# A four-layer graph network on one core: the scheduler learns of a shared port, the score weights read their vectors from PSUM, and bias times degree moves

## The chip, the cores and the metric

The kernel runs on one core of one Trainium2 chip. The metric is the time of one execution on the device in microseconds (us), from the start of the program to its end; the median of several executions counts. The engines of the core are TensorE (PE in the profile, with its weight loads as PEld), VectorE (DVE), ScalarE (ACT) and GpSimd (POOL). All DMAs of this kernel are issued by SyncE (SP). Each engine takes its instructions strictly in the order in which the program lists them.

## The reference

The input x holds 128 graphs of 64 nodes with 512 features, so 8192 rows. All graphs share one 64 x 64 adjacency. Four layers follow one another, and each adds its result to x and normalizes:

```
x = layernorm(x + L0(x)); x = layernorm(x + L1(x)); x = layernorm(x + L2(x)); x = layernorm(x + L3(x))

L0:  mi = x @ Wi.T;  mj = x @ Wj.T
     out = deg * (mi + b) + adj @ mj                       # deg = row sums of adj

L1:  four heads, each:  Wh = x @ W_heads[h]
     e[n, m] = leaky(Wh[n] . a1 + Wh[m] . a2), masked by adj; attn = softmax(e); h = elu(attn @ Wh)
     the four h are concatenated to 2048 features; one more such attention with W_out, a_out; elu
     ffn = relu(out @ w1 + b1) @ w2 + b2;  layernorm(ffn + out) * gamma + beta

L2, L3:  Wh = x @ W;  e = leaky(Wh @ a_src [n] + Wh @ a_dst [m]), masked; out = softmax(e) @ Wh
```

The scores never need Wh: Wh . a equals x . (W a). The kernel works out the vectors W a once, and calls them score weights.

## The kernel before

**Tiles and pairs.** 128 rows (two graphs) are one tile, and two tiles are a pair p. There are 32 pairs (NP), and each goes through all layers. Pairs are staggered, so that PE finds work of several pairs at any time. Matrix products of pair 4 and later are done as seven half-size products (`seven`, `strassen`), with the sums that this needs made by GpSimd and VectorE, and with weight parts streamed from DRAM into rings of buffers. The first four pairs (AHEAD) do layer 0 with plain matmuls instead, named `l` in the profile, since the streamed parts (`raw_w`, `raw_wo`, `raw_W`, made by `stage_stream`) are not ready yet.

**How the order is made.** No instruction is issued while the stages run. Each stage is a Python generator. `start(at, order, stage)` puts it on a heap, keyed by a nominal time in which one pair takes TURN = 107, and what it yields is added to its time. Every call such as `nc.vector.tensor_tensor` is only recorded by `Plan.note` (line 174) as a `Step`: its engine, its rank (place of recording), the steps it must follow, and the tiles it opens. Then `Plan.order` (line 207) runs a list scheduler over all steps. It keeps one clock for each engine, takes a duration for each step from `cost` (line 319), gives an engine the ready step with the lowest rank, and lets a step that opens a tile wait until a buffer of its tag is free. `play` (line 301) issues all steps in that order. So every instruction has the same line in the profile, L306, and a changed duration in `cost` can move any instruction of any engine, all on their in-order queues. The line that the reduces get, and the one of GpSimd:

```
    if name == "tensor_tensor_reduce":
        return 0.78, 0.0
    if engine == "gpsimd":
        return 0.25 + 0.0026 * size, 0.0
```

**PSUM.** One pool with one tag "b" and eight buffers, one bank each, serves all PSUM tiles.

**The start.** The adjacency is loaded, then the first x tile, the first quarter of W0T (two DMAs), the second x tile, the bias row spread over the partitions (`degb`), and the other quarters of W0T. VectorE works out `deg`, multiplies `degb` by it, makes masks, and builds `aggr`, the block matrix through which PE forms x times adjacency transposed (`axp`), in which an identity scaled by deg is folded. ScalarE copies `axp` to `ax`, GpSimd adds `degb` to x, PE does the `l` matmuls with `ax` and `w0`, VectorE adds them to x (`x<-l`), and `normalize` follows: `bn_stats` and `bn_aggr` on VectorE (`st`, `mv`), two small GpSimd steps (`rs`), one VectorE step (`sh`), one ScalarE step on x.

**Score weights of the heads.** `score_weights` (line 474) goes over the four heads h, the two score vectors s and the four row chunks c. Each step is a `tensor_tensor_reduce` on VectorE: a 128 x 512 chunk of the head's weights (`wh`) times the vector, spread over the partitions (`rows_a`), summed into one column of `wa_h`; its full product goes to `j_h`, which nobody reads. In the profile this operation is called CUSTOM_DVE_ANT_0, and DVE_READ_ACCUMULATOR2_ANT fetches its sum. After each head `head_sums` makes the four sums of `wh` on GpSimd, in place. `wa_h` is then used twice: by PE for the scores of the first two pairs (`fp`, from a transposed x, `x1Tp` and `x1T`), and by `score_rows`, which turns it over and stores it as rows in DRAM for the later pairs. The scores of layers 2 and 3 get theirs in the same way from `stage_score_rows`, as `j<-w,rows_a`, one "head" each.

**After the scores.** `attention_heads` forms the attention: `dg` on VectorE, `bc` on PE, a row of VectorE steps and one exponential on ScalarE, `pt` on PE, `aT` on ScalarE. PE multiplies x by it (`yp`), forms the head products (`stx_h`, `sty_h`) into `hT`, and later the product with W_out (`stx_o`, `sty_o`, parts `ws_wo` loaded from DRAM). The remaining stages follow in the same manner; the last pair uses `stage_last` and `stage_tile` with plain matmuls (`hidp`, `gp`, `yp`).

Of the kernel before, what the change touches and what calls it, by code (L numbers as in the profile page):

```python
# [12 lines left out]
FP = mybir.dt.float32  # L13
# [3 lines left out]
ALU = mybir.AluOpType  # L17
AX = mybir.AxisListType
PSUM = bass.MemoryType.PSUM

P = 128
# [120 lines left out]
class Step:  # L142
    def __init__(self, engine, rank):
        self.engine, self.rank = engine, rank
        self.calls, self.after, self.behind = [], set(), set()
        self.opens, self.uses = [], set()
        self.takes, self.lands = 0.0, 0.0


class Plan:  # L150
# [23 lines left out]
    def note(self, engine, name, args, kw):  # L174
        if self.joined:
            s = self.joined[0]
            assert s.engine == engine
        else:
            s = Step(engine, len(self.steps) - self.early)
            self.steps.append(s)  # L180
            if self.joined is not None:
                self.joined.append(s)
        out = [kw[k] for k in ("out", "accum_out") if k in kw] + (
            [] if "out" in kw or not args else [args[0]]
        )
        views = [(v, True) for v in out if isinstance(v, View)] + [
            (v, False)
            for v in [*args, *kw.values()]
            if isinstance(v, View) and not any(v is o for o in out)
        ]  # L190
        for v, writes in views:
            t = v.tile
            writes = writes or t.pool.space is PSUM
            if not t.seen:
                s.opens.append(t)
            else:
                s.behind.add(t.seen[0][0])
            s.uses.add(t)
            s.after.update(o for o, r, w in t.seen if (w or writes) and v.meets(r))
            t.seen.append((s, v.region, writes))  # L200
        s.after.discard(s)
        s.behind -= {s} | s.after
        s.calls.append((name, args, kw))
        takes, s.lands = cost(engine, name, args, kw, out)
        s.takes += takes

    def order(self):

        engines = ("tensor", "vector", "scalar", "gpsimd", "sync")
        free = dict.fromkeys(engines, 0.0)  # L210
        coming = {e: [] for e in engines}
        there = {e: [] for e in engines}
        wire, out = 0.0, []
        then = {s: [] for s in self.steps}
        for i, s in enumerate(self.steps):
            s.no, s.ready, s.waits = i, 0.0, len(s.after) + len(s.behind)
            for o in s.after:
                then[o].append((s, True))
            for o in s.behind:
                then[o].append((s, False))  # L220
            for t in s.uses:
                t.left += 1
            s.given = set()
            for k in set(t.slots for t in s.opens):
                k.openers.append(s)
        for k in set(t.slots for s in self.steps for t in s.opens):
            k.openers.sort(key=lambda s: -s.no)

        def late(s, e):
            return 0.0 if s.engine == e else WAIT + SLACK.get(s.engine, 0.3)  # L230

        def come(s):
            heapq.heappush(coming[s.engine], (s.ready, s.rank, s.no, s))

        def take(slots):

            while slots.queue:
                s = slots.queue[0][1]
                while slots in slots.openers[-1].given:
                    slots.openers.pop()  # L240
                if s.no > slots.openers[-1].no + NEAR:
                    return
                n = sum(t.slots is slots for t in s.opens)
                if len(slots.free) < n:
                    return
                heapq.heappop(slots.queue)
                s.given.add(slots)
                for _ in range(n):
                    end, _, last = heapq.heappop(slots.free)
                    s.ready = max(s.ready, end + late(s, None))  # L250
                    if last:
                        s.after.update(o for o, _, _ in last.seen)
                s.waits -= 1
                if not s.waits:
                    come(s)

        def want(s):

            kinds = {id(t.slots): t.slots for t in s.opens}.values()
            s.waits = len(kinds)  # L260
            if not kinds:
                come(s)
            for k in kinds:
                heapq.heappush(k.queue, (s.no, s))
            for k in kinds:
                take(k)

        for s in self.steps:
            if not s.waits:
                want(s)  # L270
        while len(out) < len(self.steps):
            at, e = min(
                (free[e] if there[e] else max(free[e], coming[e][0][0]), e)
                for e in engines
                if there[e] or coming[e]
            )
            while coming[e] and coming[e][0][0] <= at:
                s = heapq.heappop(coming[e])[3]
                heapq.heappush(there[e], (s.rank, s.no, s))
            s = heapq.heappop(there[e])[2]  # L280
            s.start, s.end = at, at + s.takes
            free[e] = s.end
            if s.lands:
                wire = max(wire, at) + s.lands
                s.end = wire + 2.0
            out.append(s)
            for o, whole in then[s]:
                t = s.end + late(o, None if s.lands else e) if whole else at
                o.ready = max(o.ready, t)
                o.waits -= 1  # L290
                if not o.waits:
                    want(o)
            for t in s.uses:
                t.left -= 1
                t.end = max(t.end, s.end)
                if not t.left:
                    heapq.heappush(t.slots.free, (t.end, t.no, t))
                    take(t.slots)
        return out
# [16 lines left out]
        return lambda *args, **kw: self.plan.note(self.name, call, args, kw)  # L316


def cost(engine, name, args, kw, out):

    size = max(math.prod(v.shape[1:]) for v in out) if out and isinstance(out[0], View) else 512
    if engine == "tensor":
        if name == "transpose":
            return size * 0.00085, 0.0

        beside = P * P // math.prod(kw["lhsT"].shape)
        return (
            size * 0.00169 if beside == 1 else 0.208 / beside + 0.0003 * size
        ), 0.0
    if engine == "sync":  # L330
        return 0.06, 0.0015 * size
    if name == "tensor_tensor_reduce":
        return 0.78, 0.0
    if engine == "gpsimd":
        return 0.25 + 0.0026 * size, 0.0
    return 0.17 + (0.0011 if engine == "vector" else 0.00085) * size, 0.0


# [1 line left out]
def gnn_stack_kernel(  # L340
# [24 lines left out]
    nc = Plan(tc)  # L365
    NT, D = x.shape
# [15 lines left out]
    psum = nc.pool(ctx, name="ps", bufs=8, space=PSUM)  # L382
# [32 lines left out]
    for k in range(KC):  # L415
        for s in range(2):
            nc.sync.dma_start(out=w0[s][:, k, :], in_=W0T[ts(s * KC + k, P), :])
        if k == 0:
            nc.sync.dma_start(out=xs[0][:, 1, :], in_=x[P : 2 * P, :])
            degb = row(b0, "degb")  # L420
# [17 lines left out]
    nc.vector.tensor_copy(adj_f, adj_i)  # L438
    deg = cp.tile([P, 1], FP, tag="deg", name="deg")
    nc.vector.tensor_reduce(deg, adj_f, AX.X, ALU.add)  # L440
    nc.vector.tensor_scalar(degb, degb, deg, None, ALU.mult)
    mask1 = cp.tile([P, N], I32, tag="mask1", name="mask1")
    nc.vector.tensor_scalar(mask1, adj_f, 0.0, None, ALU.is_le)
    mask2 = cp.tile([P, N], I32, tag="mask2", name="mask2")
# [17 lines left out]

    nc.vector.tensor_tensor(aggr[:, 1, 0, :], aggr[:, 0, 0, :], aggr[:, 0, 1, :], ALU.add)
    nc.vector.tensor_copy(aggr[:, 1, 1, :], aggr[:, 0, 1, :])


    aTg = [cp.tile([P, T, P], FP, tag=f"aTg{i}", name=f"aTg{i}") for i in range(2)]
# [6 lines left out]
    def score_weights(Ws, avecs, name, then=lambda h: None):  # L474

        n = len(Ws)
        wa = cp.tile([P, 2 * n, KC], FP, tag=f"wa_{name}", name=f"wa_{name}")
        for h in range(n):
            for s in range(2):
                for c in range(KC):  # L480
                    junk = unit.tile([P, D], BF, tag="junk", name=f"j_{name}_{s}_{h}_{c}")
                    nc.vector.tensor_tensor_reduce(
                        junk, Ws[h](c), avecs[h][:, s, :], 1.0, 0.0, ALU.mult, ALU.add,
                        accum_out=wa[:, s * n + h, c : c + 1],
                    )
            then(h)
            yield 5.0
        was[name] = wa
# [19 lines left out]
    for h in range(H):  # L508
        w = wp.tile([P, KC // 2, 7, D // 2], FP, tag=f"wh{h}", name=f"wh{h}")
        for s in range(2):  # L510
            nc.sync.dma_start(
                out=w[:, :, 2 * s : 2 * s + 2, :].rearrange("p c h o -> p c (h o)"),
# [734 lines left out]
    for p in range(NP):  # L1247
        if p < AHEAD:
            start(TURN * (0.2 * p - 1.2), 10 * p + 4, stage_first(p))
        else:  # L1250
# [4 lines left out]
        at, pace, rest = {NP - 2: (2.0, 0.8, 0.0), NP - 1: (1.3, 0.6, 0.0)}.get(  # L1255
            p, (1.42, 1.0, 5.0)
        )
# [76 lines left out]
```

## Time and profile before

| | us |
|---|---|
| median of 3 executions | 3350.42 (3348.55 to 3352.29) |
| the profiled execution, its own time | 3351.91 |
| its span | 3350.1 |
| PE busy | 3284.4 (98%) |
| DVE busy | 2432.1 (73%) |
| POOL busy | 1714.0 (51%) |
| ACT busy | 1356.2 (40%) |

The profiled execution took 1.8 us more than its span, and 1.5 us more than the median. The mean granted clock of PE was 0.992 of full speed. Busy time is summed for each engine over the whole span; idle time of an engine matters only where the end of the program waits for it. A group "out<-in x32 | 32.9, 1028" has 32 instructions that were busy for 32.9 us together, 1028 ns each in the mean; after the next bar stands the idle time just before them and what ended it.

### The profile page before, as it was taken

The page shows a single profiled execution, that of the slowest core. Times are in us where ns is not written, and L with a number is a line of the kernel's source. Part 1 is how long each engine was busy: PE and PEld are TensorE (multiplying, and loading weights), DVE is VectorE, ACT ScalarE, POOL GpSimd, SP SyncE. Part 2 cuts the span into 40 slices and gives each one's busy share as a digit, 9 for nine tenths or more (in the row PEclk, how much of TensorE's full clock was granted, in tenths as well). Part 3 has the DMA queues.
Part 4 walks back from the last instruction along what each step waited for, and adds up shares of the span by engine and source line. Part 5 has one row for each costly group of instructions (what it writes and reads, how often), then busy time and mean ns, then how long its engine had stood idle before and what let it go on. Part 6 is the DMA issues. An engine that isn't in the chain of part 4 may idle for free.

```text
span 3350.1 us, 59710 instructions
## 1 busy us (share of the span) xinstructions
PE 3284.4 (98%) x21298; PEld 2891.1 (86%) x21298; DVE 2432.1 (73%) x5698; ACT 1356.2 (40%) x3184; POOL 1714.0 (51%) x1860
## 2 busy tenths in 40 slices
PE   8899999999999999999999999999999999999997
PEld 4788988888988888989889889889888889889884
DVE  6757777777777777777776777777777777777756
ACT  1343444434443443443443443444444344434332
POOL 6754455554455554555544555544555544555432
PEclk9999999999999999999999999999999999999998
DMA  8766666666666676666676666666666666666751
GB/s 282 269 217 204 203 216 223 217 224 211 210 213 220 213 227 215 202 219 219 213 232 205 206 222 217 219 218 211 213 217 217 222 212 209 215 220 209 241 190 60
DMA packets 301063, 718.08 MB, mean 214 GB/s; under 512 B 32560, under 2 KB 41824, under 8 KB 300768
## 3 DMA queue, kind: packets, MB, share of 16 engines
q1 hardware_dynamic: 300768, 714.27, 66.2%
q8 instruction: 171, 2.80, 0.3%
q14 instruction: 124, 1.02, 0.1%
HBM read 680.82 MB, written 33.32 MB: 213 GB/s over the span
## 4 chain that ended last, share of the span: by engine, by line
PE 92%; DMA 3%; DVE 3%; issue 1%; SPq 1%; POOL 1%; ACT 0%; POOLq 0%; DVEq 0%
PE stx_h L306 13%; PE stx_o L306 13%; PE stx L306 12%; PE sty_h L306 10%; PE sty_o L306 10%; PE sty L306 9%; PE hidp L306 6%; PE yp L306 4%; PE gp L306 3%; PE stx_y L306 3%; PE sty_y L306 2%; PE axp L306 2%; PE bc L306 1%; PE op L306 1%; PE oTp L306 1%
## 5 line engine op out<-in xcount | busy, mean ns | idle before, releaser
L306 DVE CUSTOM_DVE_ANT_0 j<-x,rows 128x512 bf16<-128x512 f32 x736 | 610.2, 829 | 73.3 <-ACT x L306 36.4
L306 PE MATMUL stx_h<-ys,wh 128*128 128x128 f32 x3072 | 405.6, 276 | 2.1 <-DVE hT L306 1.6
L306 PEld LDWEIGHTS stx_h<-ys,wh 128*128 128x128 f32 x3072 | 386.7, 192 | 22.6 <-issue 9.0
L306 ACT COPY hT<-stx_h 128x256 f32<-128x256 f32 x384 | 143.0, 372 | 498.4 <-PE stx_h L306 491.4
L306 POOL TENSOR_SCALAR rs<-mv 128x1 f32<-128x1 f32 x256 | 85.5, 334 | 394.5 <-DVE mv L306 376.0
L306 ACT ACTIVATE x<-x,sh,rs 128x512 f32<-128x512 f32 x256 | 207.7, 814 | 179.0 <-DVE sh L306 177.4
L306 PE MATMUL sty_h<-ys,wh 128*128 128x128 f32 x2048 | 274.5, 277 | 0.0
L306 DVE TENSOR_TENSOR x<-stx,x 128x256 f32<-128x256 f32 x360 | 150.1, 418 | 155.6 <-PE stx L306 154.4
L306 PEld LDWEIGHTS sty_h<-ys,wh 128*128 128x128 f32 x2048 | 251.6, 192 | 12.3 <-issue 5.7
L306 PE MATMUL sty_o<-ws_wo,hT 128*128 128x256 f32 x1024 | 245.9, 383 | 6.6 <-DMA ws_wo<-d_wo 6.6
L306 PE MATMUL stx_o<-ws_wo_T,s_o 128*128 128x256 f32 x1024 | 244.5, 382 | 0.2 <-DVE who L306 0.2
L306 POOL TENSOR_TENSOR ys<-ys,t 128x256 f32<-128x256 f32 x128 | 113.0, 885 | 256.5 <-PE sty_h L306 256.3
L306 PE MATMUL hidp<-oT,w 128*128 128x256 f32 (+1 forms) x1056 | 231.8, 373 | 0.0
L306 DVE TENSOR_TENSOR hT<-sty_h,hT 128x256 f32<-128x256 f32 x256 | 107.8, 421 | 168.0 <-PE sty_h L306 141.3
L306 PEld LDWEIGHTS sty_o<-ws_wo,hT 128*128 128x128 f32 x1024 | 189.2, 191 | 32.3 <-issue 3.9
L306 PEld LDWEIGHTS hidp<-oT,w 128*128 128x128 f32 x1056 | 192.8, 190 | 23.7
L306 PEld LDWEIGHTS stx_o<-ws_wo_T,s_o 128*128 128x128 f32 x1024 | 185.7, 190 | 26.1 <-DVE who L306 2.6
L306 ACT ACTIVATE elu<-hT 128x512 f32<-128x512 f32 x256 | 153.3, 601 | 104.2 <-DVE hT L306 92.8
L306 DVE SCALAR_TENSOR_TENSOR hT<-elu,hT 128x512 f32<-128x512 f32 x256 | 173.0, 682 | 28.2 <-ACT elu L306 25.1
L306 DVE BATCH_NORM_STATS2 st<-x 128x6 f32<-128x512 f32 x256 | 176.3, 689 | 5.4
L306 POOL TENSOR_TENSOR rs<-rs,mhalf 128x1 f32<-128x1 f32 x256 | 154.2, 602 | 21.3
L306 ACT COPY ys<-yp 128x512 f32<-128x512 f32 x256 | 131.2, 606 | 82.8 <-PE yp L306 73.9
(199 smaller groups left out, 7706.6 us busy)
## 6 DMA issues: line engine op xcount, KB each, us to landing
ws_wo_T<-d_wo_T SPq DMA_DIRECT2D x256, 512.0 KB, 3.9
ws_wo<-d_wo SPq DMA_DIRECT2D x192, 512.0 KB, 3.6
ws_W_T<-d_W_T SPq DMA_DIRECT2D x248, 256.0 KB, 3.7
rows<-d_h SPq DMA_DIRECT2D x240, 256.0 KB, 4.3
ws_w_T<-d_w_T SPq DMA_DIRECT2D x112, 512.0 KB, 4.2
ws_W<-d_W SPq DMA_DIRECT2D x186, 256.0 KB, 3.6
ws_w<-d_w SPq DMA_DIRECT2D x84, 512.0 KB, 4.3
rows<-d SPq DMA_DIRECT2D x128, 256.0 KB, 4.6
```

The costliest lines, as they stand in the source:

```text
L306: getattr(getattr(self.tc.nc, s.engine), name)(*map(real, args), **{k: real(v) for k, v in kw.items()})
```

## The change

Four things are changed.

1. The scheduler gets a port. A VectorE step that reads more than one operand from SBUF is marked, and so is a GpSimd step that does so and writes more than two elements in each partition. In `order`, a marked step starts no earlier than the port is free, and holds the port for its duration. Only the order is made with this: no instruction waits for anything on account of it.
2. Durations in `cost`: 0.7 for a reduce, and 0.2 + 0.0021 x size for GpSimd. `size_of` is the old expression under a name.
3. The multiplication of `degb` by `deg` is recorded after `aggr` is built.
4. In `score_weights` two PSUM tiles are opened for all heads, one for each s. Before the four reduces of a head and an s, ScalarE copies the vector into its tile, and the reduces read it there. These are 8 copies for the heads and 2 each for layers 2 and 3.

```diff
@@ class Step @@
-        self.calls, self.after, self.behind = [], set(), set()
+        self.calls, self.after, self.behind, self.port = [], set(), set(), False
@@ Plan.note @@
         takes, s.lands = cost(engine, name, args, kw, out)
+        if engine in ("vector", "gpsimd"):
+
+            both = [v for v, writes in views if not writes and v.tile.pool.space is not PSUM]
+            s.port = len(both) > 1 and (engine == "vector" or size_of(out) > 2)
         s.takes += takes
@@ Plan.order @@
-        wire, out = 0.0, []
+        wire, port, out = 0.0, 0.0, []
...
             s = heapq.heappop(there[e])[2]
+            if s.port and port > at:
+                at = port
+            if s.port:
+                port = at + s.takes
             s.start, s.end = at, at + s.takes
@@ cost @@
+def size_of(out):
+    return max(math.prod(v.shape[1:]) for v in out) if out and isinstance(out[0], View) else 512
...
     if name == "tensor_tensor_reduce":
-        return 0.78, 0.0
+        return 0.7, 0.0
     if engine == "gpsimd":
-        return 0.25 + 0.0026 * size, 0.0
+        return 0.2 + 0.0021 * size, 0.0
@@ gnn_stack_kernel @@
     nc.vector.tensor_reduce(deg, adj_f, AX.X, ALU.add)
-    nc.vector.tensor_scalar(degb, degb, deg, None, ALU.mult)
...
     nc.vector.tensor_copy(aggr[:, 1, 1, :], aggr[:, 0, 1, :])
+    nc.vector.tensor_scalar(degb, degb, deg, None, ALU.mult)
@@ score_weights @@
+        inps = [psum.tile([P, D], FP, tag="b", name=f"a_{name}_{s}") for s in range(2)]
         for h in range(n):
             for s in range(2):
+                a = inps[s]
+                nc.scalar.copy(a, avecs[h][:, s, :])
                 for c in range(KC):
                     junk = unit.tile([P, D], BF, tag="junk", name=f"j_{name}_{s}_{h}_{c}")
                     nc.vector.tensor_tensor_reduce(
-                        junk, Ws[h](c), avecs[h][:, s, :], 1.0, 0.0, ALU.mult, ALU.add,
+                        junk, Ws[h](c), a, 1.0, 0.0, ALU.mult, ALU.add,
                         accum_out=wa[:, s * n + h, c : c + 1],
                     )
```

All instructions of the changed kernel are issued at its line 314.

## The prediction

> **What bounds the kernel now.** I read the page's busy shares and chain first:
>
> ```profile
> span 3350.1 us, 59710 instructions
> ...
> PE 3284.4 (98%) x21298; PEld 2891.1 (86%) x21298; DVE 2432.1 (73%) x5698; ACT 1356.2 (40%) x3184; POOL 1714.0 (51%) x1860
> ...
> PE 92%; DMA 3%; DVE 3%; issue 1%; SPq 1%; POOL 1%; ACT 0%; POOLq 0%; DVEq 0%
> ```
>
> PE is idle for 65.7 us in all. The table of busy time by stretch says where:
>
> ```profile
> core 0: us, PE busy (x) PEld busy (x) DVE busy (x) ACT busy (x) POOL busy (x), PEclk, DMA share, GB/s
> 0.00:50.00 50.00, 38.89 (x185) 21.50 (x185) 28.58 (x68) 9.66 (x16) 26.40 (x33) 1.00 0.96 330
> 50.00:100.00 50.00, 40.62 (x127) 21.77 (x128) 34.97 (x56) 9.06 (x19) 39.33 (x32) 0.85 0.59 208
> 100.00:150.00 50.00, 41.01 (x375) 38.33 (x374) 39.38 (x66) 23.38 (x51) 40.76 (x25) 0.94 0.83 285
> ...
> 400.00:3200.00 2800.00, 2798.02 (x18465) 2499.89 (x18465) 2074.74 (x4902) 1166.91 (x2739) 1434.79 (x1576) 1.00 0.68 216
> ...
> 3300.00:3350.00 50.00, 33.87 (x122) 22.36 (x121) 24.12 (x75) 13.08 (x32) 9.94 (x21) 0.78 0.11 39
> ```
>
> From 400 to 3200 PE idles 2.0 us, at full clock. Nothing that VectorE gains there can shorten the span. The first 150 us hold 11.1 + 9.4 + 9.0 = 29.5 us of idle, and lose more by a clock of 0.85 and 0.94. The last 150 hold about 29. So this change can act on the head, hardly on the tail. What PE waits for in the head (the waits of PE, 0 to 150: total, times, longest):
>
> ```profile
> PE bc L306 <- DVE dg L306: 5.3, 1, 5.3
> ...
> PE sty_o L306 <- DMA ws_wo<-d_wo: 3.7, 1, 3.7
> PE fp L306 <- DVE wa_h L306: 3.7, 4, 2.4
> ```
>
> wa_h is what the score weights write. VectorE's timeline shows the two other facts that matter (start, length, what, and the idle time before it):
>
> ```profile
> 10.30 0.49 DVE L306 TENSOR_SCALAR degb<-degb,deg 128x512 f32<-128x512 f32 x1 [4.46 <-DMA degb<-in_b_dram]
> 10.70 0.25 DVE L306 TENSOR_SCALAR aggr<-ident,deg 128x64 f32<-128x64 f32 x1
> ...
> 34.95 0.69 DVE L306 CUSTOM_DVE_ANT_0 j_h<-wh,rows_a 128x512 bf16<-128x512 f32 x1
> ...
> 42.14 0.68 DVE L306 TENSOR_TENSOR x<-l,x 128x512 f32<-128x512 f32 x1
> ...
> 55.18 1.63 DVE L306 CUSTOM_DVE_ANT_0 j_h<-wh,rows_a 128x512 bf16<-128x512 f32 x1
> ```
>
> First, VectorE sits 4.46 us in front of degb's DMA with aggr, all of PE's first work, behind it. Second, one reduce j_h takes 0.69 us or 1.63.
>
> **What the Trainium skill says.** "SBUF — State Buffer", section "Who interferes with whom": VectorE's second SBUF operand comes through an interface shared with GpSimd, and whoever has it blocks the other fully. This trace agrees: at 55.18, beside GpSimd's `wh` sums, a reduce of two SBUF operands takes 1.63 us; at 42.14, also beside such sums, the `x<-l` with one operand in PSUM takes 0.68. "Perfetto Trace Analysis", section "Optimizing Scalar/DVE Operations", gives VectorE about 65 ns more per access to PSUM (32 reduces: 2.1 us); the trace shows 0.68 against 0.69, and I follow it. "TensorE: Matmul & The Clock Gate", section "What's actually happening": an idle PE falls to half rate, a busy one regains it; the 0.85 above agrees, so idle time saved pays a little more than once.
>
> **The change, part by part.**
>
> *degb moved* (one VectorE step of 0.49; no DMA moved). The aggr steps end at about 6.2 in place of 11.3: aggr's copies from abd_ps were over at 5.8, and 0.25 + 0.23 + 0.19 overlap to 0.6. PE starts axp at 6.2 instead of 11.0. Its second tile lands at 8.4 and w0's second quarter at 10.8 to 11.6, the fourth at 14.1 (DMA answers), so PE is then near the wire. I take 4.0, ends 2 and 4.8. degb's next reader is GpSimd's x+degb, at 13.2 before: not late.
>
> *Vectors in PSUM.* 32 reduces for the heads took 32.9 us and 2.5 of accumulator reads, 35.4. At 0.69 + 0.08 with some overlap (starts in a row are 0.74 apart) they take 32 x 0.74 = 24: 11 less. Two PSUM banks of eight are held for the heads until the last reduce; the scheduler's order already has that. ScalarE gets 8 + 2 + 2 copies of 128x512 from SBUF to PSUM; nearest row, same direction:
>
> ```profile
> L306 ACT ACTIVATE elu<-hT 128x512 f32<-128x512 f32 x256 | 153.3, 601 | 104.2 <-DVE hT L306 92.8
> ```
>
> 12 x 0.6 = 7.2 us, on an engine busy 9.66 of the first 50. Cover: each head's copies run in the 6.9 us of a layer-0 tile's matmuls. Behind them in ScalarE's order stand the ax copies that feed PE. A copy for head h+1 waits for the four reduces of head h on the same bank and for its row DMA (21.8, 25.7, 29.6, 33.3 for the four heads). Following the new orders with these durations, ax of pair 1 is copied by 29 and pair 2 by 43, when PE needs them near 29 and 44. Cost 0 when on time; up to 15 if not (rival 2).
>
> wa_h is then finished not by reduces but by VectorE's in-order steps between them: `sh_2_0` waits for pair 2's first tile, and two reduces follow. I get 61 in place of 70. In the new order of PE the score products of pair 0 stand between pair 3's two layer-0 tiles, no longer ahead of both, so the 3.7 us of fp waits go and pair 3 begins near 62, not 74.3: 12 earlier.
>
> What is late next: POOL. Its order has the sums of the streamed weights (2.35 for 128x1024, 1.27 for 128x512) between its head sums and `rs_3_1`. From 50.6, without idle, I add up 33 us: rs_3_1 at 84. Its shift, then the attention of pair 0 (seven VectorE steps of about 0.7, one of which I let collide at 2.1) put PE's first `yp` at 94.6 instead of 101.6. So of the 12, 7 remain; ends 5 and 12.
>
> *The score weights of layers 2 and 3.* Their 16 reduces took 20.3 us:
>
> ```profile
> L306 DVE CUSTOM_DVE_ANT_0 j<-w,rows_a 128x512 bf16<-128x512 f32 x16 | 20.3, 1270 | 2.6 <-DMA w<-in_W_dram 2.4
> ```
>
> Eight stood at 99 to 118, ahead of the additions that PE's head products wait for (1.2, 1.1 and 1.6 us near 131 to 138, and half clock in 149.7 to 153.1). They now come after pair 0's third head. The ws_wo load comes ahead of some stores in SP's order and has landed by about 118 while PE asks at 128: the wait of 3.7 goes. Together 10.7 us can go; I take 7, ends 3 and 9.
>
> *The planner* (port time, 0.78 to 0.70, gpsimd costs) works only through the order. PE's matmuls are the same set. I compared the new order with the old for re-use of PSUM accumulators and buffers: nowhere is PE given less work between a product and its next use than before. In 400 to 3200 the most it can gain is 2.0; I put 0, from -2 to +6, since one reordered wait per pair costs 28 times. The last 75 us of PE and VectorE are in the same order: 0, from -3 to +3.
>
> **Sum.** 7 (which contains degb's 4.0, since pair 0's chain begins there) + 7 = 14. The profiled execution took 3351.9 (span 3350.1 and 1.8 around it); 3337.9 after. It stands 1.5 above the median of 3350.4, so the forecast is 3336. About 0.2%, 6.7 us, is what a measurement of this kernel tells from no change.
>
> **Rivals.**
> 1. *GpSimd is the bound of the head.* Its chain to rs_3_1 takes longer than 33 us (sums beside VectorE took 2.72 and 1.78, alone 2.35 and 1.27), and the freed ws_wo wait becomes a wait for sums: gain 5 to 8, 3344. For: the 4.11 us that rs waited at 97 was for VectorE, not POOL, so POOL has had slack; against: fewer collisions now. 0.18.
> 2. *ScalarE is blocked (slower).* A copy waits for the reduces of the head before, these stand behind `x<-l` in VectorE's order, and the ax copies wait with them. PE then idles in layer 0 of pairs 1 to 3: up to 3 x 5 us and 5 of half clock, less the 14: 3356. It decides if VectorE reaches head 0's last reduce later than 27, or head 1's later than 43. My walk has 29.5 for the former's second bank (not needed by the next ax) and 40, so 3 us of room. 0.07.
> 3. *The operand in PSUM doesn't free the port.* Reduces stay at 1.03, only degb's 4 us remain: 3346. Against: 0.68 at 42.14, and the mean of 682 ns for `hT<-elu,hT`, one operand in PSUM, over 256 instances. 0.08.
> 4. *The steady order is worse.* Each of the 28 pairs after the first four loses 0.5 us to a new wait: 14 in, 14 out, or slower if the head gives little. Against: my comparison of the orders. 0.03.
>
> **How the numbers follow.** Forecast (10 to 18 less): 0.64. With rival 1 split about evenly at 6.7, faster by over 0.2% has 0.64 + 0.12 = 0.76, within 0.2% 0.06 + 0.08 = 0.14, slower 0.07 + 0.03 = 0.10. The sum of the low ends (5 + 3 - 3) is 5, of the high ends 12 + 9 + 5 = 26; the range 3324 to 3352 leaves out one in ten on each side, the slower cases above it.
>
> **What would show it.** Right: axp starts near 6; the 32 j_h take 22 to 24 us at about 690 ns; fp no longer waits for wa_h; `yp` starts near 95; sty_o no longer waits for ws_wo; PE idle in 0 to 150 falls to about 17; 400 to 3200 as before. Wrong: j_h above 0.9 us (rival 3); PE waiting for ax or ScalarE for VectorE (rival 2); `sh_3_1` waiting for POOL beyond 85 (rival 1); more than 4 us of idle in 400 to 3200.

## The result, and the profile after

The changed kernel takes 3345.48 us (median of 20 executions, 3340.62 to 3350.72), against 3351.68 us (20 executions) for the kernel before on the same chips: a ratio of 0.9981, 95% interval 0.9974 to 0.9987, so 6.2 us less. The forecast was 14 less. The profiled execution took 3347.62 with a span of 3345.8, 2.1 above the median; the two spans shown differ by 4.3.

The page of the kernel after, busy shares and chain:

```profile
span 3345.8 us, 59820 instructions
...
PE 3284.4 (98%) x21298; PEld 2888.7 (86%) x21298; DVE 2420.4 (72%) x5698; ACT 1363.8 (41%) x3196; POOL 1684.7 (50%) x1860
...
PE 93%; DVE 2%; DMA 2%; POOL 2%; issue 1%; ACT 0%; SPq 0%; POOLq 0%; DVEq 0%
```

Idle of PE is 3345.8 - 3284.4 = 61.4, against 65.7. That small difference hides a large gain and a large loss, which the table by stretch shows: the kernel after, then 150 to 400 of the kernel before, which the prediction leaves out (from and to in us, length, busy time of PE, PEld, DVE, ACT and POOL with their instructions, granted clock, DMA share, GB/s):

```profile
0.00:50.00 50.00, 44.27 (x192) 23.58 (x193) 29.12 (x83) 15.39 (x25) 26.16 (x39) 1.00 0.96 337
50.00:100.00 50.00, 40.69 (x192) 24.00 (x191) 30.08 (x48) 13.55 (x30) 37.30 (x30) 0.83 0.81 290
100.00:150.00 50.00, 49.10 (x408) 46.21 (x407) 17.07 (x40) 24.13 (x57) 46.78 (x37) 1.00 0.90 325
150.00:200.00 50.00, 46.03 (x290) 41.17 (x290) 35.80 (x88) 21.48 (x51) 20.50 (x16) 0.97 0.65 210
200.00:450.00 250.00, 240.46 (x1568) 211.84 (x1568) 180.32 (x409) 95.00 (x225) 117.95 (x130) 0.99 0.62 201
450.00:3200.00 2750.00, 2746.55 (x18114) 2453.97 (x18113) 2042.30 (x4795) 1149.83 (x2695) 1391.78 (x1543) 1.00 0.66 215
```

```profile
150.00:400.00 250.00, 245.10 (x1586) 217.69 (x1585) 166.76 (x369) 101.05 (x240) 128.05 (x129) 0.99 0.64 210
```

Idle of PE by stretch, as length less busy time, with two of the experiments' kernels for later use. Each column is one profiled execution, which took up to 3.6 us more than its kernel's median, so differences of a few us between columns are indications only:

| PE idle, us | before | after | vectors alone (e2) | mix (e13) |
|---|---|---|---|---|
| 0 to 150 | 29.5 | 15.9 | 18.4 | 18.6 |
| 150 to 450 | 4.9 | 13.5 | 8.3 | 2.7 |
| 450 to 3200 | 2.0 | 3.4 | 2.1 | 1.7 |
| 3200 to the end | 29.4 | 28.6 | 29.0 | 29.9 |
| PE busy in all | 3284.4 | 3284.4 | 3280.1 | 3278.4 |
| span | 3350.1 | 3345.8 | 3337.8 | 3331.3 |

The head gained 13.6; 10.0 of it were given back between 150 and 3200. PE's matmuls are the same set in all four, so a difference in the row "PE busy" is taken as time that they ran at a lower clock: the changed kernel has as much of that as the kernel before, though it idles less. Its clock rose from 0.94 to 1.00 in 100 to 150, but is 0.83 against 0.85 in 50 to 100, and 0.99 against 1.00 in 200 to 450.

The three things that the prediction looked for in the head, in the kernel after (timeline of PE, then groups of VectorE and ScalarE):

```profile
6.18 4.05 PE L314 MATMUL axp<-aggr,x 64*128 64x128 f32 x32 [0.84 <-DVE aggr L314]
...
93.50 6.12 PE L314 MATMUL yp<-aT,x 64*128 64x128 f32 x64 [0.84 <-ACT aT L314]
```

```profile
L314 DVE CUSTOM_DVE_ANT_0 j_h<-wh,a_h 128x512 bf16<-128x512 f32 x32 | 21.8, 681 | 3.0 <-ACT a_h L314 2.0
```

```profile
L314 ACT COPY a_h<-rows_a 128x512 f32<-128x512 f32 x8 | 4.7, 592 | 18.6 <-DMA rows_a<-in_a_heads_dram 11.7 <-DVE wa_h L314 6.8
```

axp starts at 6.18, yp at 93.5, and every reduce takes 0.65 to 0.69 us, whatever GpSimd does. The copies cost 0.59 each; ScalarE waits 18.6 us ahead of them, but PE waits for none of the ax copies behind them.

And the waits of PE, first from 0 to 200, then from 200 to 450. The one for dg was there before (5.3); the others shown are new or larger:

```profile
PE bc L314 <- DVE dg L314: 5.7, 1, 5.7
...
PE stx_o L314 <- ACT who L314: 2.7, 1, 2.7
PE wap_h L314 <- DVE wa_h L314: 2.1, 1, 2.1
```

```profile
PE pt L314 <- DVE e L314: 5.4, 2, 4.3
...
PE stx_o L314 <- DVE who L314: 0.8, 1, 0.8
```

The wait for wa_h has thus not gone from the head: it moved from `fp` to `wap_h`, the step that turns wa_h over, and fell from 3.7 to 2.1. The first large new one stands near 190. PE needs the accumulator that the copy `who<-stx_o` empties, and that copy is behind two tiles' elu of the same pair in ScalarE's order (timelines of ScalarE and PE):

```profile
189.47 0.60 ACT L314 ACTIVATE o<-op 128x512 f32<-128x512 f32 x1
190.10 0.63 ACT L314 ACTIVATE o<-o 128x512 f32<-128x512 f32 x1
190.64 0.58 ACT L314 ACTIVATE o<-op 128x512 f32<-128x512 f32 x1
191.25 0.63 ACT L314 ACTIVATE o<-o 128x512 f32<-128x512 f32 x1
191.78 0.35 ACT L314 COPY who<-stx_o 128x256 f32<-128x256 f32 x1
```

```profile
192.19 2.98 PE L314 MATMUL stx_o<-ws_wo_T,s_o 128*128 128x256 f32 x8 [2.73 <-ACT who L314]
```

The larger one stands at 427: PE's `pt` waits for an attention whose VectorE steps are interleaved with sixteen steps of other stages (timeline of VectorE, with the attention's first step, two others, and its last; then of PE):

```profile
416.90 0.66 DVE L314 TENSOR_TENSOR e<-bc,f 128x512 f32<-128x512 f32 x1
...
419.67 1.47 DVE L314 SCALAR_TENSOR_TENSOR bc<-e 128x512 f32<-128x512 f32 x1
...
425.30 0.66 DVE L314 TENSOR_REDUCE mx<-bc 128x8 f32<-128x512 f32 x1
...
430.03 0.69 DVE L314 TENSOR_TENSOR e<-bc,r 128x512 f32<-128x512 f32 x1
```

```profile
424.62 1.99 PE L314 MATMUL stx_o<-ws_wo_T,hT 128*128 128x256 f32 x8 [0.85 <-DVE who L314]
430.87 0.63 PE L314 MATMUL pt<-ident,e 128*128 128x128 f32 x4 [4.25 <-DVE e L314]
```

13.8 us from first to end for a chain that takes 6.0 at 85.43 to 91.40 of the same kernel. PE was ready at 426.6 and began `pt` at 430.87.

### The profile page after: what moved, and what is told of

It reads as the page before. It is cut to its first block, busy times and chain, and to the rows that moved or that the text cites. A ratio compares the mean times of both kernels' runs of the same rounds, so it can differ in the third digit from the quotient of the medians.

```text
span 3345.8 us, 59820 instructions
## 1 busy us (share of the span) xinstructions
PE 3284.4 (98%) x21298; PEld 2888.7 (86%) x21298; DVE 2420.4 (72%) x5698; ACT 1363.8 (41%) x3196; POOL 1684.7 (50%) x1860
## 4 chain that ended last, share of the span: by engine, by line
PE 93%; DVE 2%; DMA 2%; POOL 2%; issue 1%; ACT 0%; SPq 0%; POOLq 0%; DVEq 0%
PE stx_h L314 13%; PE stx_o L314 13%; PE stx L314 12%; PE sty_h L314 10%; PE sty_o L314 10%; PE sty L314 9%; PE hidp L314 5%; PE yp L314 4%; PE gp L314 3%; PE stx_y L314 3%; PE sty_y L314 2%; PE axp L314 2%; PE bc L314 1%; DMA rows<-d_h 1%; PE op L314 1%; PE l L314 1%
## 5 line engine op out<-in xcount | busy, mean ns | idle before, releaser
L314 DVE CUSTOM_DVE_ANT_0 j<-x,rows 128x512 bf16<-128x512 f32 x736 | 627.9, 853 | 53.5 <-DMA rows<-d_h 23.0
L314 PEld LDWEIGHTS stx_h<-ys,wh 128*128 128x128 f32 x3072 | 392.0, 192 | 16.3 <-issue 0.9
L314 POOL TENSOR_SCALAR rs<-mv 128x1 f32<-128x1 f32 x256 | 70.8, 277 | 501.9 <-DVE mv L314 492.0
L314 DVE TENSOR_TENSOR x<-sty,x 128x512 f32<-128x512 f32 (+1 forms) x180 | 100.1, 556 | 87.2 <-PE sty L314 84.1
```

The costliest lines, as they stand in the source:

```text
L314: getattr(getattr(self.tc.nc, s.engine), name)(*map(real, args), **{k: real(v) for k, v in kw.items()})
```

## Experiments

Each kernel was timed beside the kernel before on its own chip, so ratios to it are compared, with 95% intervals. Two theories at first: **A**, the two edits of the data path (degb, vectors in PSUM) pay in the head and the planner gives part back later; **B**, the planner's new order is what pays. **C**: an earlier head by itself makes new waits. Later ones (D, E, A') are stated in the expectations that test them.

### One part alone

**e1_degb**: the one line moved.

```diff
     nc.vector.tensor_reduce(deg, adj_f, AX.X, ALU.add)
-    nc.vector.tensor_scalar(degb, degb, deg, None, ALU.mult)
...
     nc.vector.tensor_copy(aggr[:, 1, 1, :], aggr[:, 0, 1, :])
+    nc.vector.tensor_scalar(degb, degb, deg, None, ALU.mult)
```

> The kernel before with degb's multiplication moved behind the build of aggr, nothing else. Theory A (the two data-path edits pay in the head, the new planner gives part of it back later): PE's axp starts at 6.2 instead of 11.0, and of these 4.8 us about 3 reach the end, since the wa_h wait of the scores still follows contended reduces: 2 to 4 us faster. Rival B (what counts is the new planner's order, the edits alone do little): within 1 us of before, the idle saved at 5 to 11 us comes back as a longer wait of fp for wa_h.

Measured: 3352.22 against 3353.39, 0.9995 (0.9987 to 1.0003): nothing that can be told. axp started at 6.2, and the gain was gone before the first `yp`, which came at 103.1 (101.6 before). It went in two steps. The first two `l` groups of matmuls end 4.4 us earlier than before (at 25.2 and 42.9), but the third starts only 1.9 earlier, at 48.5: PE waits 3.45 us for VectorE's `x`, which stands behind reduces of up to 1.64. When that group ends, 0.2 is left. The longer wait of `fp` for wa_h, which B expected, isn't in this kernel.

**e2_psum**: the two PSUM tiles, the copies, the operand; nothing else.

```diff
+        inps = [psum.tile([P, D], FP, tag="b", name=f"a_{name}_{s}") for s in range(2)]
...
+                nc.scalar.copy(a, avecs[h][:, s, :])
...
-                        junk, Ws[h](c), avecs[h][:, s, :], 1.0, 0.0, ALU.mult, ALU.add,
+                        junk, Ws[h](c), a, 1.0, 0.0, ALU.mult, ALU.add,
```

> The kernel before with the score weights' vectors in PSUM, nothing else. Theory A: the 32 j_h take about 23 us at 0.70 each in place of 32.9, fp no longer waits for wa_h, 5 to 8 us faster. Rival B: the reduces get as fast, but the old durations place the GpSimd sums and the reduces of layers 2 and 3 where they delay the attention of pair 0; within 2 us of before.

Measured: 3338.40 against 3353.39, 0.9957 (0.9945 to 0.9970), 15 us faster: about twice the upper end of what was expected, and faster than the whole change. First `yp` at 86.3. The groups of its VectorE:

```profile
L306 DVE CUSTOM_DVE_ANT_0 j_h<-wh,a_h 128x512 bf16<-128x512 f32 x32 | 21.8, 680 | 1.3
```

**e3_planner**: `Step.port`, its use in `order`, and the durations; degb and the reduces as before.

```diff
+            if s.port and port > at:
+                at = port
+            if s.port:
+                port = at + s.takes
...
-        return 0.78, 0.0
+        return 0.7, 0.0
...
-        return 0.25 + 0.0026 * size, 0.0
+        return 0.2 + 0.0021 * size, 0.0
```

> The kernel before with the port in the planner and the new durations, nothing else; degb and the reduces as before. Theory A: the head gains nothing, PE gets the waits that the changed kernel has from 150 to 450 and the short sty_h waits for ScalarE's hT later on (together about 10 us): 3 to 9 us slower, PE idle in 400 to 3200 of 6 us or more. Rival B: the port-aware order is what pays: 4 to 7 us faster.

Measured: 3368.86, 1.0048 (1.0035 to 1.0061), 15.5 us slower, and idle of PE from 450 to 3200 of 12.2: theory B falls, and A's price for the planner was too low. Its waits of PE from 450 on are small and of many kinds, and none stands out:

```profile
PE sty_h L314 <- POOL t L314: 2.7, 3, 0.9
PE stx_o L314 <- DVE who L314: 2.5, 6, 0.5
PE sty_y L314 <- DMA ws_w<-d_w: 2.5, 5, 0.7
```

**e4_degb_psum**: e1 and e2 together, which is the change without the planner's part.

> The kernel before with degb moved and the vectors in PSUM, planner and durations as before. Theory A: idle of PE in 0 to 150 falls from 29 to 16 or so as in the changed kernel, and nothing is given back later: 400 to 3200 idles 2 to 3 us, 10 to 13 us faster, so faster than the changed kernel too. Rival B: 0 to 4 us faster; rival C (an earlier head by itself shifts the staggered pairs so that new waits appear between 150 and 450, whatever the planner): head as in A, but 6 to 10 us of new idle between 150 and 450, 4 to 7 us faster.

Measured: 3340.30, 0.9959 (0.9945 to 0.9973), 13 us faster. A holds for the planner: leaving it out is worth about 7 us by the ratios (5 by the medians; the interval ends at 0.9973, the change's begins at 0.9974). The two edits of the data path thus bring 13 of the 14 us that were forecast for the whole change. C holds in part: idle of 10.0 from 150 to 450, where before has 4.9 and the change 13.5. The waits of 0.85 and 4.25 at 424 to 431 are not in this kernel; near 190 to 195 there is one too, though another: `oTp` waits 3.4 for VectorE's `o`. The kernel also shows where degb's gain goes (timeline of ScalarE, then PE):

```profile
61.74 0.81 ACT L306 ACTIVATE x<-x,sh,rs 128x512 f32<-128x512 f32 x1 [11.62 <-DVE sh L306]
62.46 1.05 ACT L306 COPY ax<-axp 128x512 f32<-128x512 f32 x2
```

```profile
10.82 15.95 PE L306 MATMUL l<-w,ax 128*128 128x512 f32 x32
...
63.57 7.13 PE L306 MATMUL l<-w,ax 128*128 128x512 f32 x16 [2.10 <-ACT ax L306]
```

PE starts 4.6 earlier than in e2, but the first `l` group takes 15.95 where e2's took 14.00; 1.75 remain at its end. Why it took longer isn't shown: it took 14.56 in e1, which starts as early, and 14.92 in the kernel before, which starts late. Then ScalarE waits 11.62 for pair 2's `sh` with pair 3's ax copies behind it, and PE waits 2.10: nothing is left.

### The planner's two halves, and the hold of the port

**e5_no_port**: the change without the four lines in `order`; durations new.

```diff
-            if s.port and port > at:
-                at = port
-            if s.port:
-                port = at + s.takes
```

> The changed kernel with the port taken out of the planner (the steps no longer wait for it in the order), the new durations kept. Theory A (the port's time in the planner is what costs): the waits of PE between 150 and 450 fall back from 13.5 us to the 8 that the vectors and degb alone had, 3338 to 3341. Rival D (the new durations of GpSimd and of the reduce are what costs, since they place GpSimd's sums ahead of the small steps that normalization waits for): stays at 3344 to 3348.

Measured: 3342.22, 0.9970 (0.9959 to 0.9982). It lies 3 to 4 us below the change, between the ranges of A and D, and the intervals overlap. Its profile: 7.0 of idle from 150 to 450, as A has it; but 9.3 from 450 to 3200, in waits for GpSimd and for x:

```profile
PE sty_h L310 <- POOL t L310: 4.3, 3, 1.4
PE yp L310 <- DVE x L310: 3.2, 7, 0.5
```

So the durations have a price of their own there, and rival D is not wholly wrong.

**e6_old_costs**: the change with the old durations, port kept.

```diff
-        return 0.7, 0.0
+        return 0.78, 0.0
-        return 0.2 + 0.0021 * size, 0.0
+        return 0.25 + 0.0026 * size, 0.0
```

> The changed kernel with the port in the planner, but the old durations (0.78; 0.25 + 0.0026 x size). Theory A: with longer holds of the port the plan holds more engine time apart than before, and the order is worse than the changed kernel's: 8 to 30 us slower than it, with PE idle spread over all pairs from 400 to 3200. Rival D: the durations are what costs, and without them it is faster than the changed kernel, 3336 to 3341.

Measured: 3464.25, 1.0334 (1.0318 to 1.0349): 112 us slower than before and some 118 slower than the change, in A's direction but far outside its 8 to 30; D falls in its plain form. From 400 on the same few waits recur in many pairs:

```profile
PE gp L314 <- ACT aTg L314: 23.1, 25, 1.2
PE pt L314 <- DVE e L314: 21.7, 15, 4.2
PE stx_h L314 <- DVE r L314: 11.0, 12, 0.9
```

All three end in the steps of an attention. PE's busy time grew as well, for the same number of matmuls (page of this run, against 3284.4 before):

```profile
PE 3335.9 (96%) x21298; PEld 2919.9 (84%) x21298; DVE 2376.9 (69%) x5698; ACT 1358.0 (39%) x3196; POOL 1714.7 (49%) x1860
```

The idle time is 63.1 us more than before, the busy time 51.5 more, at a mean clock of 0.985 against 0.992.

e4, e5, the change and e6 are the four combinations of port and durations with the same data path:

| port | durations | kernel | ratio | PE idle, 150 to 3200 | PE busy |
|---|---|---|---|---|---|
| no | old | e4 | 0.9959 | 11.9 | 3282.8 |
| no | new | e5 | 0.9970 | 16.3 | 3279.3 |
| yes | new | the change | 0.9981 | 17.0 | 3284.4 |
| yes | old | e6 | 1.0334 | 78.2 | 3335.9 |

With the old durations the port costs some 125 us. With the new ones it costs about 4, and the new durations alone cost about 4; neither of these two is clear of noise; their sum just is. Taking the port out of the change (e5) also left PE about as much idle after 150 as with it; what fell is PE's busy time.

**e9_inplace**: the port mark counts every SBUF operand. As changed it compares views with the output and leaves out those that are the same object, so `x+degb` or a sum of streamed weights written over its first operand counts one read and isn't marked.

```diff
-            both = [v for v, writes in views if not writes and v.tile.pool.space is not PSUM]
+            both = [
+                v for v in [*(args if "out" in kw else args[1:]),
+                            *(v for k, v in kw.items() if k not in ("out", "accum_out"))]
+                if isinstance(v, View) and v.tile.pool.space is not PSUM
+            ]
```

> The changed kernel, but the port mark counts every operand read from SBUF. As changed, a step that reads and writes the same view (x+degb, the sums of the streamed weights, some of the Strassen sums on GpSimd) counts one read too few and isn't marked. Theory A (every use of the port in the order costs): slower than the changed kernel by 5 to 20 us, PE idle in 400 to 3200 of 10 us or more. Rival E (the port in the order is right in itself and only its gaps hurt, as sh stuck 2.29 us beside an unmarked raw_wo sum at 83): faster than the changed kernel by 2 to 6 us, idle in the head below 16.

Measured: 3387.59, 1.0104 (1.0090 to 1.0118), some 41 us slower than the change; idle from 450 to 3200 of 26.4. E falls. The `sh` that E names, of pair 3's second tile, does take 0.16 in place of 2.29, but the seven before it are as slow as in the change (two of 2.29 again), and around it VectorE and GpSimd have the same steps in the same order in both kernels. Here `sh` began 0.10 ahead of the sum, there 0.07 behind it; that the mark did this isn't shown. VectorE and GpSimd in the change, then in this kernel:

```profile
83.22 2.29 DVE L314 SCALAR_TENSOR_TENSOR sh<-mv,rs 128x1 f32<-128x1 f32 x1 [1.47 <-POOL rs L314]
```

```profile
83.15 2.34 POOL L314 TENSOR_TENSOR raw_wo<-raw_wo,raw_wo 128x1024 f32<-128x1024 f32 x1
```

```profile
83.75 0.16 DVE L318 SCALAR_TENSOR_TENSOR sh<-mv,rs 128x1 f32<-128x1 f32 x1 [1.31 <-POOL rs L318]
```

```profile
83.85 2.35 POOL L318 TENSOR_TENSOR raw_wo<-raw_wo,raw_wo 128x1024 f32<-128x1024 f32 x1
```

One avoided collision of 2 us in the head brought nothing: `yp` came at 93.4, as in the change.

**e14_half_hold**: the port held for half a step.

```diff
-                port = at + s.takes
+                port = at + 0.5 * s.takes
```

> The changed kernel with a port hold of half a step's duration in the planner. Theory A' (the hold as changed is too long: a reduce of 0.69 and a sum of 1.27 that meet are both over after 1.63 to 1.72, so less than the sum of both is lost): PE idle between 200 and 450 falls from 9.5 to 5 and 450 to 3200 stays below 4; 3336 to 3341. Theory A in its plain form (any hold costs): 3342 to 3346.

Measured: 3341.76, 0.9966 (0.9954 to 0.9979). The time is at the border of the two. Idle from 200 to 450 fell to 2.2 as A' says, but 7.6 from 450 on is more than its 4 (a `yp` wait of 0.46 in every second pair or so). So a shorter hold moved the loss rather than ending it. Inconclusive on the right length.

**e16_port_from_450**: the port obeyed only from 450 of the planner's clock.

```diff
-            if s.port and port > at:
+            if s.port and at >= 450.0 and port > at:
```

> The changed kernel, with the port obeyed in the planner only from 450 of its own clock on. If the port costs where pairs 0 to 4 fill the pipeline (PE's waits of 0.85 and 4.25 at 424 to 431 of the changed kernel): PE idle from 200 to 450 falls from 9.5 to about 4 as without the port, 3340 to 3342. If it costs in every pair: 3344 to 3347 as the changed kernel, with idle from 450 on of 3 us or more.

Measured: 3342.89, 0.9973 (0.9963 to 0.9982). The time lies between the two ranges. Idle from 200 to 450 fell to 3.8 as expected, but idle from 450 on rose to 10.4, though the port is obeyed there as in the change. The loss isn't tied to the filling of the pipeline: an order that differs in its first part has other waits in its steady part too.

### Which reduces, and a better mix

**e11_heads_only** and **e12_late_only**: the vectors in PSUM only for the heads, or only for layers 2 and 3.

```diff
+        inps = None
+        if name == "h":
+            inps = [psum.tile([P, D], FP, tag="b", name=f"a_{name}_{s}") for s in range(2)]
...
+                a = avecs[h][:, s, :]
+                if inps:
+                    a = inps[s]
+                    nc.scalar.copy(a, avecs[h][:, s, :])
```

e12 has `!=` in its place.

> The kernel before with the vectors in PSUM for the four heads only; the reduces of layers 2 and 3 read SBUF as before. The prediction's split: the heads bring half or more. Of the 15 us that the vectors brought in all, 8 to 12 then remain (3340 to 3344). If instead the reduces of layers 2 and 3 are what mattered, since they stand before the additions that PE waits for near 131 to 138: 2 to 5 us.

> The kernel before with the vectors in PSUM for layers 2 and 3 only; the heads' reduces read SBUF. By the prediction's split: 3 to 7 us faster, with the idle of PE from 100 to 150 down from 9.0 to 4 or less and the fp wait for wa_h still there. If the heads carry all: within 2 us of before.

Measured: heads 3345.19, 0.9980 (0.9972 to 0.9988), 7.4 us; late 3347.74, 0.9984 (0.9978 to 0.9991), 4.9 us. Both count, the heads a little under their range. The late ones do bring the idle of 100 to 150 from 9.0 to 1.8, with the fp wait of 3.6 still there. The two sum to 12.3, e2 had 15.0; by the intervals that may be the same. (The profiled execution of heads only is 5.4 slower than its median, so its idle times are not compared.)

**e10_psum_costs**: e2 with the new durations.

> The kernel before with the vectors in PSUM and the new durations; no port, degb as before. Theory A: the durations do no harm, and degb is worth nothing: equal to the vectors alone within 3 us, 3335 to 3341. Rival D: 3344 to 3348 as the changed kernel.

Measured: 3339.97, 0.9967 (0.9954 to 0.9979), within A's range. By the ratios it is about 3 us behind e2, with intervals that overlap. By its profile the durations trade, as in e5: idle from 100 to 150 of 0 (e2: 3.1), from 450 on of 8.6 (e2: 2.1).

**e13_mix**: e4 with GpSimd's short duration for the 700 steps recorded first, which are those of the head.

```diff
+LONE = 700
...
         takes, s.lands = cost(engine, name, args, kw, out)
+        if engine == "gpsimd" and len(self.steps) < LONE:
+            takes -= 0.05 + 0.0005 * max(math.prod(v.shape[1:]) for v in out)
```

> The kernel before with degb moved, vectors in PSUM, no port, and GpSimd's shorter duration (0.2 + 0.0021 x size) only for the first 700 recorded steps, the old one after them. Theory A with the durations right where GpSimd runs alone (the head: 1.27 for 128x512) and too short where it shares the port (the steady pairs): 400 to 3200 idles 2 us as with the old durations instead of 9.3, and the head is as with the new ones: 3333 to 3337, the fastest. If the order of the steady part does not depend on that: 3339 to 3343 as the two parents.

Measured: 3329.45, 0.9933 (0.9921 to 0.9946), 23 us faster than before, the lowest median of all; its interval just touches e2's. Its table by stretch:

```profile
50.00:100.00 50.00, 37.02 (x151) 20.77 (x151) 32.76 (x46) 11.21 (x25) 39.33 (x30) 0.83 0.89 317
100.00:150.00 50.00, 50.00 (x435) 47.06 (x434) 19.37 (x45) 27.38 (x61) 44.88 (x36) 1.00 0.82 300
150.00:200.00 50.00, 48.72 (x316) 43.76 (x316) 34.32 (x85) 20.89 (x50) 18.99 (x16) 1.00 0.64 204
200.00:450.00 250.00, 248.58 (x1663) 221.78 (x1662) 189.62 (x433) 102.31 (x247) 128.78 (x136) 1.00 0.65 210
```

Its head is no better than e2's (50 to 100 idles 13.0, one wait of 8.5 for an attention, `yp` at 97.1). What it has is 100 to 450: 2.7 of idle at full clock, where e2 has 11.4 and the change 14.4. 450 on idles 1.7, as with the old durations. That half of the expectation held; "the head as with the new ones" holds only from 100 on.

**e15_mix_no_degb**: e13 with degb back in its old place.

> e13_mix with degb's multiplication back in its old place. The prediction counted 4.0 us for moving degb; moved alone it was worth 1 us, within the noise. If its gain is real but was eaten in those orders (ScalarE's ax copies queued behind the activation of pair 2), it shows here, where that wait is small: 3332 to 3335, 3 to 5 us slower than e13_mix. If it is worth nothing in any order: 3327 to 3331.

Measured: 3332.47, 0.9942 (0.9929 to 0.9956). That is 3 us slower than e13, in the range for a real gain, but the two intervals overlap widely. What degb is worth stays open; it is at most a few us.

## Why the prediction was wrong

**What held.** PE's idle in 0 to 150 was to fall to about 17: 15.9. axp near 6, reduces at about 690 ns for 22 to 24 us in all (681; 21.8 without the accumulator reads), no fp wait for wa_h, `yp` near 95 (93.5), no sty_o wait for ws_wo in the head: all as said, but for what took the place of two of these waits, 2.1 of `wap_h` for wa_h and 0.9 of `stx_o` for ws_wo_T. The shared port was read rightly from the trace and from the Trainium skill's "SBUF — State Buffer", section "Who interferes with whom": one operand in PSUM frees a reduce from GpSimd entirely (681 ns in the mean of 32, many beside sums, and 690 at most, where the kernel before has up to 1680). That ScalarE's order would not hold up the ax copies (rival 2) held as well. The new time lies in the range, and rival 1's number, 3344, is nearest, but not by its mechanism: GpSimd's order did hold `rs_3_1` to 83 (84 was said), and that was already in the forecast. That the time lands near rival 1's number is chance.

**The step that failed: the planner at 0.** The prediction took the steady order's effect as 0 after comparing how soon PSUM accumulators are used again. That comparison looks at PE's own spacing. It cannot see what stands ahead of the freeing step in ScalarE's or VectorE's order, and there the new waits are: `who<-stx_o` behind elu at 190, `e` behind sixteen others at 427, `hT` behind reduces later (2.8 us in five waits). Measured: the planner's part costs about 7 us on top of the two edits (e4 to the change), and 15.5 alone (e3). The prediction's own sign of being wrong, more than 4 us of idle in 400 to 3200, came true: it is 8.6, of which 5.1 stand at 424 to 431. There is no single place: taking the port away before 450 moved the idle behind 450 (e16), a shorter hold did too (e14), and a fuller mark or longer durations multiplied it (e9, e6). Shown is that more port time than in the change makes the order worse. Less of it, or none, gains 3 to 4 us, which isn't clear of noise, and doesn't bring e4's low idle back, since the new durations have waits of their own. Why the greedy order reacts so was not tried.

**The head's gain was counted as if nothing followed.** The kernel without planner changes (e4) saves 12.4 us of idle in 0 to 150, and even it gives 5.1 back between 150 and 450 (10.0 against 4.9). That the staggered pairs then meet in another order is the likely reason; it isn't shown.

**The clock term.** "Idle time saved pays a little more than once", drawn from the Trainium skill's "TensorE: Matmul & The Clock Gate", section "What's actually happening", didn't show in the change: PE is busy for 3284.4 as before, with a clock of 0.83 in 50 to 100. It does show in other kernels of this case. e2 has 4.3 less busy time, with 8.0 less idle. e6 and e9 have 63.1 and 19.0 more idle than the kernel before, and 51.5 and 16.2 more busy time for the same matmuls, so about 0.8 us for each us of idle. But e3 has 15.8 more idle and no more busy time, and e13 has 6.0 less busy time with a wait of 8.5 in it. What decides this isn't shown.

**degb at 4.0.** Off in size: 1 us alone, within noise. Its low end, 2, was argued from w0's wire, but the wire took little in e1, where 4.4 of 4.8 were left after the first two `l` groups; in the change the first group ends at 25.1 against 28.5 in e2. What took the rest is in-order waiting farther on: for VectorE's `x` behind slow reduces in e1, for ScalarE's ax copies behind an activation in e4, and mostly for wa_h in the change, where pair 3's `l` start at 62.6 against 63.1 in e2.

**The vectors.** Undersized: together with degb they were to give 14, and alone gave 15, split 7.4 and 4.9 when taken apart (7 minus degb, and 7, in the prediction). That both edits together brought 13 of 14 is in part luck: one term was too high and the other too low.

**The sums.** The planner's term had a bad end of +6, but the sum of the low ends, 5 + 3 - 3, takes only the tail's -3. With it the sum is -1, close to what the upper end of the range, 3352, stands for. Of the waits "near 131 to 138", the one of 1.6 stands at 108.3. The four waits named with it sum to 7.6, not 10.7; that leaves 3.1 to a stretch of 3.4 us at half clock, which can cost 1.7 at most. And rival 1's chance is split 0.12 to 0.06, not about evenly. These slips move the ends of the forecast, not its middle.

## What to carry to other kernels

Where an order of instructions is computed, every change of a modelled duration or resource is a change of the whole program: price it by looking for waits in every stretch and on every in-order queue, not only where the edit is aimed. A more faithful resource in a greedy scheduler can make a worse order; try it apart from the edits that it comes with, and keep the old model where the old order was already almost without waits (e13). Moving one of two SBUF operands of VectorE to PSUM is cheap when ScalarE has room, and it makes the step's time independent of GpSimd.

## What was not expected of the hardware

A VectorE step of 128x1 with two SBUF operands that starts just after a GpSimd sum takes as long as the sum: `sh` took 2.29 us beside one of 2.34, 1.21 beside one of 128x512 (1.3), and 0.16 where it started ahead of the sum (e9). So in these traces the block lasts for the whole GpSimd instruction, and small steps lose most by ratio. In the first 80 us of the change, seven of them cost 9.3 us:

```profile
L314 DVE SCALAR_TENSOR_TENSOR sh<-mv,rs 128x1 f32<-128x1 f32 x7 | 9.3, 1334 | 10.0 <-POOL rs L314 10.0
```
